# Two transformer layers on one core: gathers that add into x, rows that travel with their weights, an inverse root on VectorE, heads by halves, VectorE in program order in the feed-forward

## The chip, the core and the metric

The kernel runs on one core of a Trainium2 chip. The metric is the device time of one execution in microseconds (us). Six queues matter: TensorE (PE in the profile, its weight loads PEld), VectorE (DVE), ScalarE (ACT), GpSimd (POOL), and the issuing of DMAs by SyncE (SP), ScalarE and POOL. Each works its own instructions in order; semaphores hold an instruction, and all that is queued behind it on the same engine, until its inputs are there.

## The reference

Two pre-norm layers run one after the other on x of shape (2, 1024, 128), float32:

```
x = x + latent_attention(layernorm(x))      # 8 heads, no mask
x = x + experts(layernorm(x))               # 8 experts + 1 shared, top 2 of each token, hidden 352
x = x + causal_attention(layernorm(x))      # 16 heads of 8, rotary
x = x + chosen_mlp(layernorm(x))            # 2 of 8 MLPs for a whole sequence, chosen by its row 0

layernorm(x) = (x - mean) / sqrt(var + 1e-5)
experts(y)   = ffn_shared(y) + sum over the token's 2 experts e of w_e * ffn_e(y)
ffn(y)       = (silu(y @ gate) * (y @ up)) @ down
```

The two weights w_e of a token are its two largest softmax probabilities of the gate, divided by their sum.

## The kernel before

The planner. The kernel is written for a tile framework. It records instructions in program order; then a planner simulates the engines and puts each engine's instructions in an order: an engine that is free takes the ready instruction that is first in program order. `tc.manual_schedule(engines=...)` leaves the named engines in program order instead. Before the change only TensorE is named. Generators make the program order: each `yield` ends a step, `zip_longest` or `beside(main, extras)` takes one step of each generator in turn, `after(n, g)` lets n steps pass first, and `spread(g, n)` makes one step of g into n.

First attention. Four passes' worth of work (2 sequences x 2 groups of 4 heads) run two deep: pass i computes the row maxima of unit i (`maxima0`, scores L513, reduce L517) beside the exponentials and sums of unit i-1 (`attend0`: scores L581 and L587, exp L592, values L612). The sums of exponentials (L597, L600) are formed by POOL, 12 tensors of 128x1024 in each half of a pass; the last unit's by VectorE (`adder`). At the end of a half `den` (L629) needs the sums. Pass i = 3 has 32 steps of this, and beside it `route(0)`; pass 4 has only `attend0(3)`.

`route(b)` prepares the experts of sequence b: layer norm (`layernorm_steps`, keeping the normed rows `xn`), gate logits, softmax, `top2`, ranks of the tokens within their experts (a matmul with a triangle), and from these the place `pos` of each (token, choice) in a list of 23 blocks of 128 rows that is sorted by expert. Then 16 indirect DMAs on POOL (L339; 8 tiles of tokens, 2 choices) scatter the rows `xn` into `xs` in DRAM. All write the same DRAM tile, so each waits for the one before to land. `xs` was filled with zeros at the start.

`layernorm_steps` uses `rsqrt` (L138 to L146): a power of -1/2 on POOL (L140) and one Newton step on VectorE.

Feed-forward. `blocks(b)` runs through the 23 blocks: load (`xb`, L749) of four blocks at a time from `xs`, transpose, then three stages that lie one step apart: `up(j)` (L770, silu L775, product L776), `mid(j-1)` (transposes L783, copy L787), `down(j-2)` (L798, copy to `yb` L803); `yb` goes to `ys` in DRAM by SP (L806). 25 steps. `shared(b)` is the shared expert (L717 to L734), which adds into x. `combine(b)` gathers the two rows of each token from `ys` into one of 6 buffers `yg` (L832, POOL) and adds each, times its weight, into x on VectorE (L841). The order is: blocks(0) with the last quotients of the attention and route(1) beside it; shared(0), blocks(1), shared(1) with `start` (combine(0), heads(0), fetch(0)) and the first maxima of the second attention beside them; then combine(1).

Second attention. `heads(b)` makes layer norm, q and k with rotary, splits each into three bfloat16 parts (copy on ScalarE L915, subtraction on POOL L918) and stores them in `parts` in DRAM by SP (L916). `fetch(i, queue)` loads the operands `qp` and `kp` of head group i from there (L941, 72 rows). `maxima(i)` (L967, reduce L977) finds the row maxima; `send` writes them by way of DRAM into three more rows of qp (`md<-mt` L985, `qp<-md` L986), and `kp` has ones there. `attend(i)` (scores L1065, exp L1070, mask on POOL L1074, values L1090) contracts over all 128 rows, the rest being zeros in qp and ones in kp (memsets L872, L873). Pass i has maxima(i) beside attend(i-1); `choose` picks the MLPs (indirect DMAs L1153 and the bias sum L1163 on POOL), and `finish` does output projection and MLP for half a sequence. `heads(1)` runs beside pass 1.

Of the kernel before, what the change touches and what calls it, by code (L numbers as in the profile page):

```python
# [3 lines left out]

# [6 lines left out]
F32 = mybir.dt.float32  # L11
BF16 = mybir.dt.bfloat16
I32 = mybir.dt.int32
# [24 lines left out]
MASKED = -(2.0 ** 100)  # L38


@with_exitstack
def two_layers(ctx: ExitStack, tc: tile.TileContext, a: dict, out: bass.AP):
# [47 lines left out]
    mhalf = const.tile([P, NT], F32, name="mhalf")  # L90
    nc.vector.memset(mhalf, -0.5)

# [12 lines left out]
    def layernorm_steps(b, bank, xt, keep=None, halves=(0, 1)):  # L105
# [3 lines left out]
        for n in range(4 * halves[0], 4 * halves[-1] + 4):  # L109
            nc.vector.bn_stats(stats[:, n, :], x[:, b * NT + n, :])  # L110
            nc.vector.bn_aggr(mv[:, n, :], stats[:, n, :])
        rstd = rsqrt(mv[:, 4 * halves[0] : 4 * halves[-1] + 4, 1], 4 * len(halves))
        for half in halves:
            xns = []
            for i in range(4):
                n = 4 * half + i
                m = n - 4 * halves[0]
                if keep is None:
                    xn = small.tile([P, D], F32, name="xn", bufs=4)
                else:  # L120
                    xn = keep[:, n, :]
# [4 lines left out]
                xns.append(xn)  # L126
            yield
            tp = bank()
            for i in range(4):
                nc.tensor.transpose(tp[:, i * P : (i + 1) * P], xns[i], ident)  # L130
            h = half - halves[0]
            nc.any.tensor_copy(xt[:, h * 512 : (h + 1) * 512], tp)
        yield

    def rsqrt(v, n):

        var = small.tile([P, n], F32, name="var")
        nc.vector.tensor_scalar(var, v, LN_EPS, None, ALU.add)  # L138
        rstd = small.tile([P, n], F32, name="rstd")
        nc.gpsimd.tensor_tensor(rstd, var, mhalf[:, 0:n], ALU.pow)  # L140

        fix = small.tile([P, n], F32, name="fix")
        nc.vector.tensor_mul(fix, rstd, rstd)
        nc.vector.tensor_mul(fix, fix, var)
        nc.vector.tensor_scalar(fix, fix, -0.5, 1.5, ALU.mult, ALU.add)
        nc.vector.tensor_mul(rstd, rstd, fix)  # L146
# [58 lines left out]
    xs_d = [tc.dram_tile([NBLK * P, D], F32, name=f"xs{b}") for b in range(B)]  # L205
# [42 lines left out]
    def route(b, bank):  # L248


        xn = rt.tile([P, NT, D], F32, name="xn")
        xt = xt_pool.tile([P, S], F32, name="xt")
        yield from layernorm_steps(b, bank, xt, xn)
        lg = bank()[:, 0 : NT * NE].rearrange("p (n e) -> p n e", e=NE)
        for n in range(NT):
            nc.tensor.matmul(
                lg[:, n, :], xt[:, n * P : (n + 1) * P], gate_w, start=True, stop=True
            )
        top = small.tile([P, NT], F32, name="lmax")
# [76 lines left out]
        routed[b] = xt, poss, base, vs  # L336
        for n in range(NT):
            for k in range(2):
                nc.gpsimd.indirect_dma_start(  # L339
                    out=xs_d[b],  # L340
                    out_offset=bass.IndirectOffsetOnAxis(
                        ap=poss[k][:, n : n + 1], axis=0
# [989 lines left out]
```

## Time and profile before

| what | value |
|---|---|
| three runs | 1080.73, 1082.16 and 1087.71 us; median 1082.16 |
| the profiled execution | 1080.86 us, its span 1079.0 us, mean granted TensorE clock 0.916 |
| TensorE busy | 888.1 us, 82% of the span |
| VectorE, ScalarE, POOL busy | 588.7, 431.5, 399.2 us |
| first layer norm to the last denominator of the first attention | 24.5 to 478.7 us |
| blocks(0) | first expert matmul at 480.1 us |
| blocks(1) | first expert matmul at 599.2 us |
| second attention | first score of attend(0) at 718.4 us |

The span runs from the first to the last instruction of one execution; what the metric has beyond it (1.9 us) lies around it. Busy time leaves out the issuing of DMAs. "Granted clock" is the share of TensorE's full clock that it was given. A line in the profile's order of time has start, duration, engine, source line, operation, tiles and, in brackets, how long the engine stood idle before it and what ended that.

### The profile page before, as it was taken

What the parts mean: (1) busy time and instruction counts of PE and PEld (TensorE: products, weight loads), DVE (VectorE), ACT (ScalarE), POOL (GpSimd) and SP (SyncE); (2) the same over time, 40 slices, a digit from 0 to 9 for tenths busy, and PEclk for the clock granted to TensorE, in tenths of its full rate; (3) what the DMA queues carried; (4) which work ended last, traced back from release to release, by engine and by line L of the source; (5) the groups of instructions that cost most, each with busy time, mean ns of one, the idle gap of its engine ahead of it and who ended that gap; (6) DMA issues with size and microseconds to landing.
All of it is one profiled execution on the core that took longest, in us unless ns stands there. A gap on an engine that the chain in (4) does not pass through costs nothing.

```text
span 1079.0 us, 14251 instructions
## 1 busy us (share of the span) xinstructions
PE 888.1 (82%) x5244; PEld 422.4 (39%) x5244; DVE 588.7 (55%) x1060; ACT 431.5 (40%) x720; POOL 399.2 (37%) x491
## 2 busy tenths in 40 slices
PE   3999999999978776996993889768558898879984
PEld 2423353433323222334762556333224344434333
DVE  3496554555665843666512432586436676647532
ACT  0103334443422332653530345115356665656661
POOL 4005546548453573005037141524623321423420
PEclk9899999999988997999896899869769999969998
DMA  9400000000000000012111223303121222130000
GB/s 271 118 1 1 1 2 1 1 1 1 1 1 1 10 20 10 1 30 69 30 52 49 62 81 94 62 17 64 21 60 33 35 37 46 28 44 13 3 1 20
DMA packets 41047, 37.47 MB, mean 35 GB/s; under 512 B 6067, under 2 KB 38227, under 8 KB 39827
## 3 DMA queue, kind: packets, MB, share of 16 engines
q1 hardware_dynamic: 34896, 28.40, 11.4%
q0 software_dynamic: 2848, 5.58, 1.9%
q10 hardware_dynamic: 3235, 2.58, 1.0%
q8 instruction: 42, 0.69, 0.3%
q14 instruction: 26, 0.21, 0.1%
HBM read 24.03 MB, written 12.52 MB: 34 GB/s over the span
## 4 chain that ended last, share of the span: by engine, by line
PE 56%; DVE 16%; POOL 9%; issue 9%; DMA 5%; ACT 3%; POOLq 0%; SPq 0%; ACTq 0%; DVEq 0%
PE sc L581 9%; PE sc L513 7%; PE up L1090 6%; PE ud L612 5%; PE banks L967 5%; DVE mx2a L517 4%; PE bank L1065 4%; PE gub L770 3%; DVE mx L977 3%; POOL xs L339 2%; PE sc L587 2%; DVE rden L639 2%; PE yblk L798 2%; PE den L629 1%; DMA yg<-ys,pos 1%
## 5 line engine op out<-in xcount | busy, mean ns | idle before, releaser
L977 DVE TENSOR_REDUCE mx<-banks 128x2 f32<-128x1024 f32 (+3 forms) x160 | 173.5, 1114 | 85.8 <-PE banks L967 42.7
L592 ACT ACTIVATE ex<-sc 128x1024 f32<-128x1024 f32 x128 | 131.1, 1024 | 218.2 <-PE sc L587 216.0
L517 DVE TENSOR_REDUCE mx2a<-sc 128x2 f32<-128x1024 f32 x128 | 153.7, 1219 | 99.5 <-PE sc L513 92.1
L1070 ACT ACTIVATE ex<-bank 128x512 f32<-128x512 f32 (+2 forms) x320 | 156.6, 557 | 123.2 <-PE bank L1065 115.2
L581 PE MATMUL sc<-q,key 64*128 64x512 f32 x512 | 141.8, 617 | 20.6 <-DVE mx2a L517 20.4
L600 POOL TENSOR_TENSOR sum<-sum,ex 128x1024 f32<-128x1024 f32 x60 | 140.4, 2354 | 38.9 <-ACT ex L592 38.7
L513 PE MATMUL sc<-key,q 64*128 64x512 f32 x512 | 149.5, 638 | 1.2 <-DVE mx2a L517 1.1
L1065 PE MATMUL bank<-qp,kp 128*128 128x512 bf16 (+3 forms) x384 | 98.0, 343 | 38.7 <-DMA qp<-md 31.1
L1074 POOL TENSOR_SCALAR_AFFINE_SELECT ex<-ex 128x128 f32<-128x128 f32 (+1 forms) x192 | 62.8, 332 | 176.3 <-ACT ex L1070 171.7
L967 PE MATMUL banks<-kp,qp 72*128 72x512 bf16 (+3 forms) x384 | 107.2, 351 | 17.8 <-DVE mx L977 14.9
L581 PEld LDWEIGHTS sc<-q,key 64*128 64x128 f32 x512 | 49.7, 190 | 89.3 <-issue 44.3
L597 POOL TENSOR_TENSOR sum<-ex,ex 128x1024 f32<-128x1024 f32 x12 | 28.1, 2348 | 144.9 <-ACT ex L592 144.9
L513 PEld LDWEIGHTS sc<-key,q 64*128 64x128 f32 x512 | 48.5, 191 | 70.5 <-issue 41.0
L1090 PE MATMUL up<-ex,vp 128*32 128x512 f32 (+3 forms) x768 | 75.0, 508 | 0.8 <-POOL ex L1074 0.8
L770 PE MATMUL gub<-wall,xbt 128*128 x184 | 66.3, 487 | 5.0 <-DVE hds L776 3.7
L612 PE MATMUL ud<-ex,val 128*32 128x512 f32 x512 | 69.4, 614 | 0.0
L967 PEld LDWEIGHTS <-qp 72*128 72x128 bf16 x384 | 38.9, 104 | 55.1 <-issue 40.8
L776 DVE TENSOR_TENSOR hds<-slb,gub 128x352 f32<-128x352 f32 x46 | 23.7, 519 | 63.3 <-ACT slb L775 63.1
L1065 PEld LDWEIGHTS <-kp 128*128 128x128 bf16 x384 | 32.7, 100 | 62.9 <-DMA qp<-md 33.3
L639 DVE RECIPROCAL rden<-us 128x128 f32<-128x128 f32 x32 | 28.3, 923 | 48.1 <-ACT us L633 48.1
L339 POOL DMA_INDIRECT xs<-xn,pos x32 | 32.0, 1001 | 60.4 <-DMA xs<-xn,pos 28.3
L587 PE MATMUL sc<-mr,onesb 64*128 64x512 bf16 x256 | 52.0, 384 | 0.0
(247 smaller groups left out, 1132.4 us busy)
## 6 DMA issues: line engine op xcount, KB each, us to landing
qp<-parts SPq DMA_DIRECT2D x72, 64.0 KB
kp<-parts SPq DMA_DIRECT2D x63, 64.0 KB
parts<-qk SPq DMA_DIRECT2D x24, 128.0 KB
xs<-zeros SPq DMA_DIRECT2D x10, 256.0 KB
xb<-xs SPq DMA_DIRECT2D x10, 256.0 KB
ys<-yb SPq DMA_DIRECT2D x10, 256.0 KB
wall<-in_ffn_gate_dram SPq DMA_DIRECT2D x1, 1584.0 KB
wall<-in_ffn_up_dram SPq DMA_DIRECT2D x1, 1584.0 KB
```

The lines of the kernel that those rows point to most:

```text
L513: nc.tensor.matmul(sc[:, j, :], qs[i][pr][r, st * P : (st + 1) * P], key2[r, 512 * c : 512 * (c + 1)], start=True, stop=True,)
L517: nc.vector.tensor_reduce(mx2[:, 2 * pr : 2 * pr + 2, st, c], sc, AX.X, ALU.max, negate=True,)
L581: nc.tensor.matmul(sc[:, j, :], key2[r, k * P : (k + 1) * P], qs[i][pr][r, cols], start=True, stop=False,)
L592: nc.scalar.activation(ex, sc, AF.Exp)
L600: adder.tensor_tensor(sums[pr], sums[pr], ex, ALU.add)
L612: nc.tensor.matmul(ud[DC * j : DC * (j + 1), :], val[:, k, :], es[j // 2][:, j % 2, :], start=(k == 0), stop=(k == NT - 1),)
L770: nc.tensor.matmul(gu[:, s, 0:FF], xbs[j // 4][:, (j % 4) * P : (j % 4 + 1) * P], flat[:, bass.ds(e0 + FF * s, FF)], start=True, stop=True,)
L967: nc.tensor.matmul(sc[:, n, 0:w], qp[0:KP, j, s0 : s0 + P], kp[0:KP, j, c0:c1], start=True, stop=not diag,)
L977: nc.vector.tensor_reduce(to, sc[:, :, 0:w], AX.X, ALU.max, negate=True)
L1065: nc.tensor.matmul(sc[:, j, 0:w], kp[:, j0 + j, t0 : t0 + P], qp[:, j0 + j, lo:hi], start=True, stop=True,)
L1070: nc.scalar.activation(ex[:, :, 0:w], sc[:, :, 0:w], AF.Exp, scale=SCALE1)
L1090: nc.tensor.matmul(up[WH * j : WH * (j + 1), lo - c0 :], vps[b][:, k, h : h + WH], es[j], start=(k == 0), stop=end,)
```

## The change

1. `rsqrt` takes a first guess by an integer shift and subtraction, and four Newton steps of three instructions, all on VectorE.
2. `xs` rows are 129 long: the normed row and its weight. `scatter(b)` copies the weights of a choice into column 128 of `xn` and scatters choice by choice. For sequence 0 it stands in pass 4 of the first attention, for sequence 1 behind route(1), two scatters a step.
3. `down` multiplies each row by its weight as it copies y to `yb` (VectorE), and `combine(b, half)` has indirect DMAs that add the gathered rows into x; `yg` and the VectorE additions go.
4. `layernorm_steps` has more steps (`lag=2` in route and heads), and its copies of the transposes run on ScalarE; route(0) starts after 4 steps and takes one step for each of the pass, route(1) starts after 4.
5. `heads(b, half, xt)` works by halves of the sequence, and its stores are issued by ScalarE.
6. VectorE too is in program order in the feed-forward (blocks(0) up to the end of combine(1)).
7. `attend` contracts over 75 rows; qp is not cleared, kp gets its ones in 32 rows, beside the gathers.
8. `xb` has four buffers; the pools of the second attention have `reuse_waits="tile"`.

```diff
+KP = 9 * DH
+ONES = float(np.uint32(0x3F803F80).view(np.float32))
...
-    def layernorm_steps(b, bank, xt, keep=None, halves=(0, 1)):
+    def layernorm_steps(b, bank, xt, keep=None, halves=(0, 1), lag=1):
...
+        for half in halves:
+            for n in range(4 * half, 4 * half + 4):
+                nc.vector.bn_stats(stats[:, n, :], x[:, b * NT + n, :])
+                nc.vector.bn_aggr(mv[:, n, :], stats[:, n, :])
+            if lag > 1:
+                yield
         rstd = rsqrt(mv[:, 4 * halves[0] : 4 * halves[-1] + 4, 1], 4 * len(halves))
+        if lag > 1:
+            yield
...
+        for _ in range(lag):
+            yield
+        for half in halves:
             tp = bank()
...
-            nc.any.tensor_copy(xt[:, h * 512 : (h + 1) * 512], tp)
+            nc.scalar.copy(xt[:, h * 512 : (h + 1) * 512], tp)
         yield

     def rsqrt(v, n):
...
+        half = small.tile([P, n], I32, name="vhalf")
+        nc.vector.tensor_scalar(half, var.bitcast(I32), 1, None, ALU.logical_shift_right)
         rstd = small.tile([P, n], F32, name="rstd")
-        nc.gpsimd.tensor_tensor(rstd, var, mhalf[:, 0:n], ALU.pow)
+        nc.vector.tensor_scalar(
+            rstd.bitcast(I32), half, -1.0, float(0x5F3759DF), ALU.mult, ALU.add
+        )
         fix = small.tile([P, n], F32, name="fix")
-        nc.vector.tensor_mul(fix, rstd, rstd)
-        nc.vector.tensor_mul(fix, fix, var)
-        nc.vector.tensor_scalar(fix, fix, -0.5, 1.5, ALU.mult, ALU.add)
-        nc.vector.tensor_mul(rstd, rstd, fix)
+        for _ in range(4):
+            nc.vector.tensor_mul(fix, rstd, rstd)
+            nc.vector.scalar_tensor_tensor(fix, fix, -0.5, var, ALU.mult, ALU.mult)
+            nc.vector.scalar_tensor_tensor(rstd, fix, 1.5, rstd, ALU.add, ALU.mult)
...
+    def scatter(b, every=1):
+        _, poss, _, vs, xn = routed[b]
+        for k in range(2):
+            nc.gpsimd.tensor_copy(xn[:, :, D], vs[k])
+            for n in range(NT):
                 nc.gpsimd.indirect_dma_start(
                     out=xs_d[b],
+                    out_offset=bass.IndirectOffsetOnAxis(ap=poss[k][:, n : n + 1], axis=0),
                     in_=xn[:, n, :], in_offset=None,
...
+                if n % every == every - 1:
+                    yield
...
                 if i == n - 1:
-                    yield from after(3, route(0, bank0))
-            passes.append(spread(more(), 4 if i < n - 1 else 2))
+                    yield from after(4, route(0, bank0))
+                if i == n:
+                    yield from scatter(0)
+            passes.append(spread(more(), 4 if i < n - 1 else 1))
...
-            nc.any.tensor_copy(ybs[gi][:, j % 4, :], y)
+            nc.vector.tensor_scalar(
+                ybs[gi][:, j % 4, :], y, xbs[gi][:, j % 4, D : D + 1], None, ALU.mult
+            )
...
-    def combine(b):
+    def combine(b, half):
+        poss = routed[b][1]
+        for k in range(2):
+            for n in range(4 * half, 4 * half + 4):
+                nc.gpsimd.indirect_dma_start(
+                    out=x[:, b * NT + n, :], out_offset=None, in_=ys_d[b],
+                    in_offset=bass.IndirectOffsetOnAxis(ap=poss[k][:, n : n + 1], axis=0),
+                    bounds_check=NBLK * P - 1, oob_is_err=True, compute_op=ALU.add,
+                )
+                if n % 2:
+                    yield
...
+    def route1():
+        yield from route(1, bank1)
+        yield from scatter(1, 2)
+
+    with tc.manual_schedule(engines={mybir.EngineType.PE, mybir.EngineType.DVE}):
+        extras = beside(blocks(0), [quotients(), after(4, route1())])
...
-    for qp, kp in qkp:
-        nc.gpsimd.memset(qp[64:P], 0.0)
-        nc.vector.memset(kp[64:P], 1.0)
...
-                    nc.sync.dma_start(parts_d[b][i, k, :, cols], h)
+                nc.scalar.dma_start(parts_d[b][i, k, :, cols], h)
...
+    def both_heads(b):
+        xt = xt_pool.tile([P, S], F32, name="xt")
+        yield from heads(b, 0, xt)
+        yield from heads(b, 1, xt)
...
+    def ones_of_keys():
+        for _, kp in qkp:
+            yield
+            nc.vector.memset(kp[64:96].bitcast(F32), ONES)
+    def start():
+        for _ in zip_longest(combine(0, 0), ones_of_keys()):
+            yield
+        for _ in zip_longest(combine(0, 1), after(4, both_heads(0))):
+            yield
         fetch(0, nc.gpsimd)
         yield
...
+    def results():
+        yield from combine(1, 0)
+        yield from combine(1, 1)
...
-                        sc[:, j, 0:w], kp[:, j0 + j, t0 : t0 + P],
-                        qp[:, j0 + j, lo:hi], start=True, stop=True,
+                        sc[:, j, 0:w], kp[0 : KP + 3, j0 + j, t0 : t0 + P],
+                        qp[0 : KP + 3, j0 + j, lo:hi], start=True, stop=True,
...
-    extras = [after(2, heads(1), 1)]
+    extras = [after(2, both_heads(1), 1)]
```

## Prediction

> **What bounds the kernel now.** I read the page's shares and chain first, then busy time by stretch, the waits of TensorE, and the order of time around each of its long waits.
>
> ```profile
> PE 888.1 (82%) x5244; PEld 422.4 (39%) x5244; DVE 588.7 (55%) x1060; ACT 431.5 (40%) x720; POOL 399.2 (37%) x491
> PE 56%; DVE 16%; POOL 9%; issue 9%; DMA 5%; ACT 3%; POOLq 0%; SPq 0%; ACTq 0%; DVEq 0%
> ```
>
> TensorE sets the end wherever it is fed; 44% of the chain is what it waits for. So a gain is only a removed wait. There are four big ones. The first stands in stretches of equal work: half a pass of the first attention (the times run from one denominator L629 to the next).
>
> ```profile
> 187.00:234.90 47.90, 47.51 (x276) 18.38 (x272) 25.80 (x33) 20.21 (x21) 28.06 (x12) 1.00 0.00 1
> 234.90:281.40 46.50, 44.75 (x269) 16.31 (x264) 28.25 (x41) 18.54 (x20) 28.00 (x12) 1.00 0.01 1
> 281.40:347.60 66.20, 53.76 (x292) 20.00 (x288) 43.37 (x81) 18.77 (x21) 29.78 (x13) 0.90 0.00 1
> 347.60:416.50 68.90, 47.69 (x270) 16.12 (x263) 33.31 (x50) 19.14 (x21) 44.30 (x28) 0.88 0.05 16
> ```
>
> The waits of TensorE in the last two of them, in total, times and longest:
>
> ```profile
> PE sc L581 <- DVE mx2a L517: 12.4, 4, 6.7
> PE den L629 <- POOL sum L600: 15.8, 2, 11.7
> ```
>
> After length come PE, PEld, DVE, ACT and POOL busy in the first fence, then the granted clock. The two halves of pass 3, with route(0) beside them, take 18 and 22 us more than their twins. In the second, POOL has 16 scatters between its 12 sums:
>
> ```profile
> 373.20 0.97 POOL L339 DMA_INDIRECT xs<-xn,pos  x1 [1.56 <-DMA xs<-xn,pos]
> 375.70 0.97 POOL L339 DMA_INDIRECT xs<-xn,pos  x1 [1.53 <-DMA xs<-xn,pos]
> 376.70 2.35 POOL L600 TENSOR_TENSOR sum<-sum,ex 128x1024 f32<-128x1024 f32 x1
> 379.22 1.00 POOL L339 DMA_INDIRECT xs<-xn,pos  x1 [0.17 <-issue]
> ```
>
> A scatter waits for the landing of the one before (1.5 us), and the sums stand behind it in POOL's queue. Second, blocks(0): three memsets sit in VectorE's queue between the layer norm's steps, and TensorE's transposes wait (a line of the order of time, then one of the waits).
>
> ```profile
> 508.65 3.47 DVE L873 MEMSET kp<- 64x4096 bf16 x1 [0.91 <-issue]
> PE bank L130 <- DVE xn L122: 10.0, 1, 10.0
> ```
>
> Third, blocks(1) waits for the last scatter of route(1), which was held up by 16 gathers on the same queue:
>
> ```profile
> 592.06 1.04 POOL L339 DMA_INDIRECT xs<-xn,pos  x1 [0.30 <-issue]
> 594.42 11.01 SPq L749 DMA_DIRECT2D xb<-xs  x4
> 597.41 1.09 PE L756 MATMUL bank<-ident,xb 128*128 128x128 f32 x4 [4.91 <-DMA xb<-xs]
> ```
>
> Fourth, early in the second attention, TensorE idles 24.3 us:
>
> ```profile
> 769.15 0.62 ACT L915 CAST qk<-ta 128x512 bf16<-128x512 f32 x1
> 783.65 1.14 POOL L918 TENSOR_TENSOR ta<-ta,qk 128x512 f32<-128x512 f32 x1
> 787.35 3.31 SPq L916 DMA_DIRECT2D parts<-qk  x4
> 790.75 0.71 SPq L986 DMA_DIRECT2D qp<-md  x1
> 793.34 1.03 PE L1065 MATMUL bank<-qp,kp 128*128 128x512 bf16 x2 [24.29 <-DMA qp<-md]
> ```
>
> The maxima rows (qp<-md) stand in SP's queue behind the stores of heads(1) (parts<-qk), these wait for ScalarE, ScalarE for POOL's subtraction, and that stands behind eight expert gathers and their sum.
>
> **The change, part by part.**
>
> *Pass 3, second half.* The scatters move in program order to pass 4, where VectorE does the sums and POOL is nearly idle (0.25 us busy from 416.5 to 480). But POOL's order is still the planner's, and it fills gaps: of the 16 scatters now, 8 stand after every sum of pass 3 in program order, yet all 16 ran before the twelfth sum. I take it that they are drawn forward again. What changes is that route's steps come closer: the rank matmuls fall in step 17 of 32, not 21, so the first scatter starts about 6 us into the half instead of 19 (366.8 - 347.6). From there to 416.4 POOL needed 49.6 us for 9 sums of 2.35 and 16 scatters, so 28.4 us for the scatters. After: 6 + 12 x 2.35 + 28.4 = 62.6 against 68.9: **-6** (ends: 0, and -22 if they stay out).
>
> *Pass 3, first half.* The layer norm is cut into steps with maxima between them, and its xt copies go to ScalarE. TensorE's longest wait here is 6.7; half of it: **-3** (0 to -7).
>
> *Inverse root.* Now 15 VectorE instructions in place of 5 and a power on POOL. By the 0.20 us from one small one to the next (L143 to L146) that is 3.0 us, where it took 2.8 for 128x8 (598.38 to 601.16) and 2.1 for 128x4. Only the last norm lies bare on the path: **+1** (0 to +4). All twelve Newton steps read two tiles in SBUF, and beside a POOL sum such an instruction takes 2.30 us at L143 and 2.26 at L144 instead of 0.17. There were just two, since POOL has no third sum while VectorE holds TensorE up; I count the same two. [...]
>
> *blocks(0), scatter(1), gathers.* T0 is the first expert matmul (480.1 now). A step of blocks takes 2.19 us. The kp memsets cover half the rows and come after blocks(0), beside gathers; POOL's qp memsets (10.4 us) go. VectorE in program order carries some 18 us of route(1) over 15 steps, 1.2 a step, with 2.19 - 0.8 free in each: no stall. route(1) needs 19 steps before its scatters: 19 x 2.19 + 1.3 (turns) + 4.2 (quotients, transposes, gate) = T0+47, now T0+57. The last yb is stored at 25 x 2.19 + 2 + 4.2 + 3 = T0+64, and the gathers may start. Scatters alone take 2.73 each (536.9 to 564.2, ten), so 6 are out by then and 10 left. Now the planner put four gathers to a scatter; so 16 gathers and 4 scatters at 1.32 (26.4), then five periods of 2.73 to the start of the last: T0+104. From that to the first matmul of blocks(1) is 7.1 (592.06 to 599.17): T0+111, now T0+119.1: **-8**. At one to one it would be T0+96 (-23).
>
> No row shows a gather that adds. Lower end: the plain gather's 1.32. Upper: the scatter's 2.73, since each second add on a tile waits for the first to land; 16 x 2.73 + 13.7 from T0+64, plus 7.1, gives T0+128.5 (+9). I take 1.32: the second add is issued four or more places later, 5.3 us, against 2.6 from issue to use now (565.48 to 568.10). Behind such a wait on POOL stand the other scatters and later the heads' sums; on VectorE the x add of shared(0) (L734) waits for the same gathers, and behind it the products of shared(0) and blocks(1). That is hidden under the scatters: 64 + 26.4 + 3 is before 111. Rows of 516 bytes change zero fill (issued by 35, used from 366), scatter and xb (fetched two groups ahead; only the first is bare): 0 to +3, taken 0. Two copies of the weights on POOL for each batch, 0.2 each by L1015, the second behind one more landing of 1.5: 0 to +4, in the scatters' own chain, taken 0. The weight moves to yb on VectorE, 0.28 instead of ScalarE's 0.27, VectorE being 30 to 45% busy there: 0, or 0.28 a block if not.
>
> *blocks(1) with heads(0), 70 us.* 12 stores go from SP to ScalarE, 0.33 each (L881) = 4 us in 70, ScalarE being under half busy; SP's xb, yb and fetches no longer stand behind them: 0 (-3 to +4).
>
> *shared(1) to attention, 669.7 to 718.4.* 16 products L841 of 0.35 leave a VectorE that is 80% busy at the end, and the gathers' waits for their buffers (710.40, 713.63) go: **-5** (-10 to +6). The pools' finer reuse waits: attention starts there right behind maxima, no wait shows, 0.
>
> *Second attention.* The power wait at 720 (TensorE idle 3.76): **-2** (0 to -4). The 24.3: without stores ahead of it, qp<-md could go at 765 (mt is done at 762.99), and TensorE at 769. But ScalarE too stood still from 769.8 to 784.8 for POOL, and 6 stores' copies stand before the next exponentials. By halves, the last chunk comes at steps 15 and 16 with buffers long free, just ahead of the expert gathers; POOL work left is 7.2 us, so a wait of 8 to 10 stays: **-14** (-22 to +3). [...] Contraction over 75 rows: 128 and 72 rows take the same (343, 351 ns), 0.
>
> Sum: -6 -3 +1 -8 -5 -2 -14 = -37. The profiled execution took 1080.9 (span 1079.0 and 1.9 around it), 1.3 under the median shown: **1044**.
>
> **Rivals.**
> A. The scatters stay out of pass 3: its second half near 47: 16 more, **1028**. For it: program order, sums first where both are ready; against: the 8 drawn forward.
> B. ScalarE goes on waiting for POOL: the 24.3 only change their name, **1058**. For it: 769.8 to 784.8; against: the chunks come earlier than the gathers.
> C. Slow adds, the slower side. With g us per adding gather, VectorE reaches blocks(1)'s first product at T0+64+16g+2 instead of T0+114 (forecast), which binds from g = 3; after blocks(1) POOL has 37 us for 16 (674.5 to the casts of maxima(0) at 711.4), which binds from 2.3. Cost 16(g-3) + 16(g-2.3). At g = 5: 32 + 43, **1119**; slower than now by 1% from g = 4.2. For it: nothing like it was measured; against: 1.32 and 2.73.
> D. It does little: mixing as at +9 and no gain in pass 3: 1044 + 17 + 9 = **1070**, with B over 1080.
>
> **How the numbers follow.** Forecast 0.50, A 0.17, B 0.17, C 0.08, D 0.08. The likeliest time is 1044; its own range, with the ends of B and scatter mixing, is 1022 to 1062. The range that leaves two in ten out reaches to A with one-to-one mixing (1028 - 15) and to D: 1010 to 1074. About 1% (1071 to 1093) can be told from no change. Forecast, A and B are faster, with a tenth of D's and B's mass lost to the middle: faster 0.83, same 0.09, slower 0.08.
>
> **What would show it.** Right: scatters between the sums of the last POOL half-pass again, that half 60 to 65; the next passes as before; no memset in blocks(0) and that stage near 62 instead of 75; blocks(1) first matmul some 111 after T0; the wait on qp<-md under 10; adding gathers 1.0 to 1.3 on POOL. Wrong: POOL idle between sums there (A); ScalarE idle over 12 us before an L1070 with POOL's subtraction named (B); L734 or products in blocks(1) waiting for the gathers for over 10 us (C); scatters still last before blocks(1) at T0+119 (D).

## The result: 36 us slower, and the profile after

The changed kernel takes 1118.1 us (median of four runs, 1118.0 to 1120.0) against 1082.2 for the kernel before: a ratio of 1.032, 95% interval 1.029 to 1.036. The forecast was 1044, and slower had a chance of 0.08. The profiled execution's span went from 1079.0 to 1116.5 us.

Engine shares and the chain of waits, from the page of the kernel after:

```profile
PE 925.0 (83%) x5244; PEld 435.4 (39%) x5244; DVE 605.1 (54%) x1209; ACT 426.8 (38%) x688; POOL 392.4 (35%) x480
PE 56%; DVE 14%; issue 13%; POOL 10%; ACT 3%; DMA 3%; POOLq 0%; SPq 0%; ACTq 0%; DVEq 0%
```

TensorE executes the same 5244 matmuls, but is busy 925 us with them where it was 888. The clock that it was granted fell: on the mean 0.881 in the profiled execution, where it was 0.916. The sum was made by stages, so the two traces are compared by stages. Busy time by stretch, cut at the first expert matmul of blocks(0) (T0), the first of blocks(1), the first score of the second attention, and the end; columns as in the prediction (length, PE, PEld, DVE, ACT, POOL, granted clock, DMA share, GB/s). The kernel before:

```profile
480.09:599.17 119.08, 81.35 (x429) 59.79 (x429) 52.17 (x143) 37.72 (x85) 47.39 (x39) 0.85 0.18 52
599.17:718.44 119.27, 101.39 (x513) 66.71 (x514) 55.31 (x105) 38.67 (x88) 37.26 (x42) 0.90 0.27 65
718.44:1079.00 360.56, 283.18 (x1992) 133.47 (x1990) 202.04 (x366) 195.44 (x382) 113.28 (x291) 0.90 0.17 31
```

The kernel after:

```profile
477.42:603.72 126.30, 82.06 (x430) 59.33 (x430) 49.65 (x149) 32.15 (x64) 41.70 (x34) 0.81 0.21 50
603.72:737.16 133.44, 100.16 (x513) 67.90 (x514) 63.58 (x162) 36.44 (x73) 45.09 (x42) 0.88 0.27 55
737.16:1116.50 379.34, 323.36 (x1992) 146.31 (x1990) 215.08 (x437) 196.47 (x382) 106.53 (x284) 0.82 0.16 29
```

| stage | before | forecast (before and its terms) | after | after over forecast |
|---|---|---|---|---|
| start to T0 | 480.1 | 472.1 (-6 -3 +1) | 477.4 | +5.3 |
| T0 to blocks(1) | 119.1 | 111.1 (-8) | 126.3 | +15.2 |
| blocks(1) to the second attention | 119.3 | 114.3 (-5) | 133.4 | +19.1 |
| second attention to the end | 360.6 | 344.6 (-2 -14) | 379.3 | +34.7 |

The table names the three places to explain. The waits of TensorE in the kernel after (in total, times, longest) give the first hints:

```profile
PE bank L777 <- DMA xb<-xs: 27.0, 2, 24.0
PE den L648 <- POOL sum L619: 18.5, 2, 18.1
...
PE tp_m L999 <- POOL mp L1035: 17.8, 6, 12.1
PE bank L1095 <- DMA qp<-md: 12.1, 5, 3.0
...
PE banks L985 <- DVE hd L744: 10.8, 2, 9.9
```

The stall that was to go has gone: the longest wait for the maxima rows (qp<-md) is 3.0 us, where it was 24.3. But blocks(1) now waits 24.0 for its rows (4.9 before), and two waits of 12.1 and 9.9 us are new.

**T0 to blocks(1).** In order of time, engines mixed:

```profile
553.11 1.55 POOL L853 DMA_INDIRECT x<-ys,pos  x1 [0.31 <-issue]
554.97 1.56 POOL L853 DMA_INDIRECT x<-ys,pos  x1 [0.30 <-issue]
...
567.27 0.69 DVE L755 TENSOR_TENSOR x<-bank,x 128x512 f32<-128x512 f32 x1 [14.73 <-DMA x<-ys,pos]
...
581.61 1.56 POOL L853 DMA_INDIRECT x<-ys,pos  x1 [0.31 <-issue]
583.48 1.07 POOL L358 DMA_INDIRECT xs<-xn,pos  x1 [0.30 <-issue]
...
585.12 0.69 DVE L755 TENSOR_TENSOR x<-bank,x 128x512 f32<-128x512 f32 x1 [11.44 <-DMA x<-ys,pos]
...
596.60 0.97 POOL L358 DMA_INDIRECT xs<-xn,pos  x1 [1.66 <-DMA xs<-xn,pos]
598.94 2.01 SPq L770 DMA_DIRECT2D xb<-xs  x4
```

An adding gather occupies GpSimd for 1.56 us, and the next one starts 1.86 us after it (553.11 to 554.97); a plain one took 1.01 and 1.32. Two plain ones of the kernel before:

```profile
572.16 1.01 POOL L832 DMA_INDIRECT yg<-ys,pos  x1 [0.30 <-DMA yg<-ys,pos]
573.48 1.01 POOL L832 DMA_INDIRECT yg<-ys,pos  x1 [0.31 <-issue]
```

The last scatters stand behind the gathers in the same queue, and blocks(1) behind the last scatter. VectorE's x add (L755) waits for the gathers twice.

**Before the second attention.** Again in order of time:

```profile
702.21 0.29 DVE L112 BATCH_NORM_STATS2 stats<-x 128x6 f32<-128x128 f32 x1 [4.51 <-DMA x<-ys,pos]
...
707.51 0.29 DVE L112 BATCH_NORM_STATS2 stats<-x 128x6 f32<-128x128 f32 x1 [1.31 <-DMA x<-ys,pos]
...
708.13 0.68 DVE L744 TENSOR_TENSOR hd<-sl,gu 96x512 f32<-96x512 f32 x1
...
725.18 1.56 POOL L853 DMA_INDIRECT x<-ys,pos  x1 [0.30 <-issue]
726.21 0.76 POOL L1033 CAST mp<-mx 128x16 bf16<-128x16 f32 x1
...
731.29 0.30 PE L999 MATMUL tp_m<-identb,mp 128*48 128x128 bf16 x1 [12.09 <-POOL mp L1035]
```

On VectorE the statistics of heads(1)'s layer norm stand ahead of the last product of shared(1), and each waits for a gather: that is TensorE's 9.9. On GpSimd the casts of the first maxima (L1033) stand among the gathers: that is the 12.1.

**Second attention.** Stretches of 4 us of the kernel after, early in one of its passes:

```profile
841.00:845.00 4.00, 4.00 (x25) 1.65 (x25) 1.74 (x3) 1.94 (x4) 0.00 (x0) 0.50 0.09 24
845.00:849.00 4.00, 4.00 (x13) 1.52 (x12) 2.82 (x3) 2.54 (x6) 0.00 (x0) 0.50 0.40 69
849.00:853.00 4.00, 4.00 (x20) 0.81 (x18) 1.32 (x2) 1.53 (x3) 0.00 (x0) 0.50 0.55 66
```

And of the kernel before, behind a like wait (its stretch from 890 to 894 has TensorE busy 1.75 of 4):

```profile
894.00:898.00 4.00, 4.00 (x28) 1.65 (x27) 1.86 (x4) 2.36 (x5) 0.00 (x0) 0.57 0.01 0
898.00:902.00 4.00, 2.83 (x19) 1.61 (x18) 3.23 (x6) 2.49 (x5) 0.00 (x0) 1.00 0.22 55
```

After some of its short waits (2.27 us until 839.41, with qp<-md named; 1.93 until 893.44 before the change) the clock falls to 0.50. In the stretch shown of before it was back at 1.00 some 4 us later; now TensorE is busy without a gap for 12 us and still gets 0.50. Counted in such stretches, the clock lies below 0.75 for 140 us of the second attention, where it was 68. This isn't seen as a wait anywhere, but as busy time: 323.4 us against 283.2.

### The profile page after: what moved, and what is told of

It is laid out like the page before. It is cut to its first block, busy times and chain, and to the rows that moved or that the text cites. A ratio compares the mean times of both kernels' runs of the same rounds, so it can differ in the third digit from the quotient of the medians.

```text
span 1116.5 us, 14367 instructions
## 1 busy us (share of the span) xinstructions
PE 925.0 (83%) x5244; PEld 435.4 (39%) x5244; DVE 605.1 (54%) x1209; ACT 426.8 (38%) x688; POOL 392.4 (35%) x480
## 4 chain that ended last, share of the span: by engine, by line
PE 56%; DVE 14%; issue 13%; POOL 10%; ACT 3%; DMA 3%; POOLq 0%; SPq 0%; ACTq 0%; DVEq 0%
PE sc L600 9%; PE sc L532 7%; PE up L1120 7%; PE bank L1095 6%; PE banks L985 5%; PE ud L631 5%; DVE mx2a L536 4%; POOL x L853 4%; PE sc L606 2%; DVE mx L995 2%; DVE rden L658 2%; POOL xs L358 2%; POOL ta L930 2%; PE gub L791 1%; PE den L648 1%
## 5 line engine op out<-in xcount | busy, mean ns | idle before, releaser
L995 DVE TENSOR_REDUCE mx<-banks 128x2 f32<-128x1024 f32 (+3 forms) x160 | 174.6, 1114 | 91.1 <-PE banks L990 67.9
L985 PE MATMUL banks<-kp,qp 72*128 72x512 bf16 (+3 forms) x384 | 116.8, 377 | 16.0 <-DVE hd L744 10.8
L1095 PE MATMUL bank<-qp,kp 75*128 75x512 bf16 (+3 forms) x384 | 108.7, 374 | 20.4 <-DMA qp<-md 12.1
L1120 PE MATMUL up<-ex,vp 128*32 128x512 f32 (+3 forms) x768 | 89.6, 579 | 2.8 <-POOL ex L1104 2.8
L853 POOL DMA_INDIRECT x<-ys,pos x32 | 50.3, 1571 | 45.7 <-DVE x L755 37.0
L985 PEld LDWEIGHTS <-qp 72*128 72x128 bf16 x384 | 41.1, 109 | 57.8 <-issue 44.5
L1095 PEld LDWEIGHTS <-kp 75*128 75x128 bf16 x384 | 35.5, 108 | 49.9 <-issue 22.7
L990 PE MATMUL banks<-mask_st,identb 128*128 128x128 bf16 x256 | 53.6, 237 | 0.0
```

What stands on the lines that cost most here:

```text
L853: nc.gpsimd.indirect_dma_start(out=x[:, b * NT + n, :], out_offset=None, in_=ys_d[b], in_offset=bass.IndirectOffsetOnAxis(ap=poss[k][:, n ...
L985: nc.tensor.matmul(sc[:, n, 0:w], qp[0:KP, j, s0 : s0 + P], kp[0:KP, j, c0:c1], start=True, stop=not diag,)
L995: nc.vector.tensor_reduce(to, sc[:, :, 0:w], AX.X, ALU.max, negate=True)
L1095: nc.tensor.matmul(sc[:, j, 0:w], kp[0 : KP + 3, j0 + j, t0 : t0 + P], qp[0 : KP + 3, j0 + j, lo:hi], start=True, stop=True,)
L1120: nc.tensor.matmul(up[WH * j : WH * (j + 1), lo - c0 :], vps[b][:, k, h : h + WH], es[j], start=(k == 0), stop=end,)
```

## Experiments

Two theories came from this. **K**: contracting the scores over 75 rows in place of 128 keeps the granted clock low for longer. **G**: the adding gather's own time is the cost in the middle. Their rivals: the clock falls because the waits have moved (I), and VectorE in program order is the cost (V).

### K against I: the rows alone, taken from the one kernel and given back to the other

```diff
 # before.py, L1065 (e1); after.py the other way round (e2)
-sc[:, j, 0:w], kp[:, j0 + j, t0 : t0 + P], qp[:, j0 + j, lo:hi]
+sc[:, j, 0:w], kp[0 : KP + 3, j0 + j, t0 : t0 + P], qp[0 : KP + 3, j0 + j, lo:hi]
```

Kernel before with 75 rows, expected:

> The kernel before, with the scores of the second attention contracted over 75 rows in place of 128 and nothing else changed (the rows left out hold zeros, so the result stays). Theory K: fewer rows keep the granted TensorE clock at 0.50 for longer after each wait of the second attention (after the change it stays there 12 to 16 us, before 4 to 8), so the time rises by 25 to 40 us, to 1107 to 1122, and the mean granted clock from 718 us on falls from near 0.92 to near 0.82. Rival I: the clock falls because of the changed waits, rows have no part in it: within 5 us of 1082.

Kernel after with 128 rows, expected:

> The kernel after, with the scores of the second attention contracted over all 128 rows again (VectorE's memsets of the keys cover rows 64 to 128, and three more, of zeros into the queries, stand beside them, where VectorE waits anyway). Theory K: the time falls by 25 to 40 us, to 1078 to 1093; the stall of 24 us that the change removed stays removed. Rival I (rows have no part in the clock): 1113 to 1123.

Measured: 1112.5 us (ratio to before 1.027, 1.023 to 1.030), so +30; and 1089.2 (1.005, 1.003 to 1.008), so -29 from the kernel after. The first one's windows show the same picture as the kernel after, with nothing else of the change in it:

```profile
838.00:842.00 4.00, 4.00 (x26) 1.66 (x22) 1.91 (x3) 2.04 (x5) 0.00 (x0) 0.50 0.10 24
842.00:846.00 4.00, 4.00 (x13) 1.52 (x11) 2.45 (x3) 2.52 (x5) 0.00 (x0) 0.50 0.39 71
846.00:850.00 4.00, 4.00 (x19) 0.61 (x17) 1.23 (x1) 1.08 (x2) 0.00 (x0) 0.50 0.53 64
```

K holds and I falls. With 128 rows the second attention of the changed kernel takes 348.2 us, 12.4 less than before the change, and TensorE is busy 291.2 us in it: of the 40 us of added busy time the rows account for 32.

### How the loss depends on the rows

The same line with 104, 88 and 96 rows, on the kernel before:

> The kernel before with the scores of the second attention contracted over 104 rows (rows left out hold zeros). If the loss grows with the rows left out (53 of 128 cost 30 us): 24 rows cost some 14, 1092 to 1100. If it comes at once with any row left out: 1107 to 1115. If 104 is enough for the clock: 1080 to 1086.

> The kernel before with the scores of the second attention contracted over 88 rows (rows left out hold zeros). If the loss sets in at once when 96 rows or fewer are used: 1107 to 1115. If it fades between 75 (1112.5) and 104 rows (1084.9) in proportion: 1096 to 1102. If it begins only below 88: 1081 to 1087.

> As the kernel beside it, with 96 rows. If the loss sets in at once when 96 rows or fewer are used: 1107 to 1115. In proportion between 75 and 104: 1090 to 1094. If it begins below 96: 1081 to 1087.

| rows | time, us | ratio to before (95%) |
|---|---|---|
| 75 | 1112.5 | 1.027 (1.023 to 1.030) |
| 88 | 1100.9 | 1.020 (1.014 to 1.025) |
| 96 | 1086.6 | 1.006 (1.003 to 1.009) |
| 104 | 1084.9 | 1.001 (0.999 to 1.002) |

104 rows cost nothing that can be measured, 96 about 5 us, 88 about 19 with runs from 1091 to 1107, 75 all 30. On the mean the loss fades out between 75 and 104 rows. 88 rows lie in the range named for a loss in proportion, 96 in the one named for hardly any. The traces show how the mean comes about, in stretches of 1 us: TensorE is busy throughout and yet at 0.50 for at most 6 us on end with 128 rows (kernel before), 8 with 104, 7 with 96, and 15 with 88 and with 75 (e1). With 88 rows some of these stretches are as short as with 128 (3 us from 838) and one as long as with 75 (15 us from 798).

### G against V: the gathers and VectorE's order

`e4` gives VectorE's order in the feed-forward back to the planner; `e3` does so too and gathers plainly, with the sums on VectorE.

```diff
-with tc.manual_schedule(engines={PE, DVE}):          # e3 and e4, twice
+with tc.manual_schedule(engines={PE}):
-    out=x[:, b * NT + n, :], ..., compute_op=ALU.add,   # e3 only
+    out=y, ...,
+nc.vector.tensor_add(x[:, b * NT + n, :], y, x[:, b * NT + n, :])
```

> The kernel after with plain gathers into buffers of their own and the sums on VectorE (weights stay in the rows), and with VectorE's order in the feed-forward left to the planner again. Theory G (the adding gather is the cost: 1.86 us from one to the next against 1.32, and its read and write of x ties it to the sums of the shared expert): the first expert matmul of blocks(1) comes 10 to 20 us earlier than now, shared(1) to attention takes about 50 in place of 62, and the time is 1085 to 1095, at least 8 below the kernel that frees VectorE's order alone. Rival V (VectorE in program order is the cost): within 5 us of that kernel.

> The kernel after with VectorE's order in the feed-forward left to the planner again, the gathers adding as they do. Theory G: blocks(1) still waits for scatters that stand behind the adding gathers on POOL, so only the wait of the layer norm's statistics ahead of the products in shared(1) goes, 10 us: 1104 to 1112. Rival V (VectorE in program order is the cost): the waits at both ends of blocks(1) go, 1090 to 1098.

Measured: e4 1122.6 (ratio to before 1.036, 1.032 to 1.039), 4.5 over the kernel after and no gain at all; e3 1091.4 (1.005, 1.002 to 1.009), 31 below e4. The 4.5 lie before T0 (482.4 against 477.4), which this edit doesn't reach; each stage behind it is within 0.3 us of the kernel after. V falls: program order was no loss. G had expected a small gain from e4 and was wrong in that: TensorE's wait of 9.9 for a product is gone, but one of 10.5 for the first maxima (PE banks L985 <- DVE mx L995) stands in its place.

What of the adding gather costs, its own time or the waits that come with writing x in place? `e13` drops the addition and keeps every wait (it is e2 with one more edit, so it stands against e2's 1089.2):

```diff
-    bounds_check=NBLK * P - 1, oob_is_err=True, compute_op=ALU.add,
+    bounds_check=NBLK * P - 1, oob_is_err=True,
```

> The kernel after with 128 rows (1089.2 us) and with gathers that overwrite x and do not add to it: the sum of the shared expert and of the first gather is left out of the result, every wait on x stays. If the instruction's own time is the cost: the gathers follow each other at 1.3 us, 16 x 0.54 = 9 us go in front of blocks(1) and as many in front of the second attention, 1069 to 1074. If the waits on x are the cost: 1083 to 1091.

Measured: 1068.6, so -20.6. Groups of GpSimd in the middle stage, first the kernel after, then e13 (columns: busy us, mean ns, idle before and its reasons):

```profile
L853 POOL DMA_INDIRECT x<-ys,pos x16 | 25.1, 1570 | 4.7 <-issue 4.7
```

```profile
L853 POOL DMA_INDIRECT x<-ys,pos x16 | 16.5, 1031 | 4.7 <-issue 4.4 <-DMA xs<-xn,pos 0.3
```

The time is lost in the instruction: 0.54 us in each of 32. In e13 blocks(1) starts 117.0 us after T0, against 125.9 with the addition (-8.9), and the next stage takes 124.3 against 133.6 (-9.3); 16 x 0.54 is 8.6. The other 3 us of the gain fall in the second attention (345.1 against 348.2) and are not explained.

### Both parts undone

The edits of e2 and e3 together are `e5b`; `e5a` is the same, but keeps VectorE in program order.

> The kernel after with both parts that proved costly undone: contraction over 128 rows, and plain gathers with the sums on VectorE, VectorE still in program order in the feed-forward. If the two losses (29 us for the rows, 27 to 31 for the adding gathers) lie in different stages and add up: 1058 to 1066, faster than the kernel before by 16 to 24. If program order makes VectorE wait for the plain gathers just as it waited for the adding ones: 1078 to 1090.

> As the kernel beside it, with VectorE's order in the feed-forward left to the planner. If the two losses add up: 1058 to 1066. If they overlap (the stall at the start of the second attention comes back when attention starts earlier): 1075 to 1090.

Measured: with VectorE in program order 1063.8 (0.984, 0.979 to 0.990), left to the planner 1068.9 (0.988, 0.983 to 0.994). With program order the two losses add up, and without them the change is a gain of 18 us. Left to the planner it is 3 over the range for that: blocks(1) starts 124.6 us after T0 there, 113.9 with program order. The better of the two is still 20 short of the forecast.

### The scatters of batch 0 (rival A)

`e6` is e5b with GpSimd added to the engines in program order, in passes 3 and 4 each by itself. The scatters stayed in pass 3 (the first at 355.7, the last at 405.6), since each pass keeps an order of its own, so 1069.9 us says nothing on A. `e8` is e5a with passes 3 and 4 under one order:

```diff
-for each pass: with tc.manual_schedule(engines={PE}): ...
+passes 3 and 4 together: with tc.manual_schedule(engines={PE, Pool}): ...
```

> The free kernel beside it, with GpSimd in program order in passes 3 and 4 of the first attention, so that the 16 scatters of batch 0 stay in pass 4, where GpSimd has no sums. The prediction priced this as rival A at 16 us (22 at most): 14 to 22 below the kernel beside it, the second half of pass 3 at 47 to 50 us, no wait of the denominators for the sums. Against it: if pass 3 is held by VectorE's maxima and not by GpSimd, under 5; if 16 scatters at 2.7 us (43) end after pass 4 has (60), nothing is lost there.

> The kernel with 128 rows and plain gathers (VectorE in program order in the feed-forward, 1063.8 us), now with GpSimd in one program order over passes 3 and 4 together, so that the 16 scatters of batch 0 come after the last sum of pass 3. (With an order for each pass by itself they stayed in pass 3: first at 355.7, last at 405.6.) Rival A as the prediction priced it: the wait of 19.3 us before a denominator goes, the second half of pass 3 takes 47 to 50 us, the time is 14 to 20 lower, 1044 to 1050. Against A: the sums end last only because VectorE's maxima and the sums share the half anyway: under 5 lower.

Measured: 1047.6 (0.968, 0.962 to 0.974), 16.3 below the same kernel without it. The two halves of pass 3 and then pass 4, e8:

```profile
280.40:345.10 64.70, 52.81 (x294) 20.29 (x289) 44.76 (x89) 19.79 (x23) 28.14 (x12) 0.92 0.00 1
345.10:397.40 52.30, 47.00 (x267) 17.18 (x263) 30.34 (x50) 18.49 (x20) 30.22 (x15) 0.93 0.01 2
397.40:455.70 58.30, 58.30 (x382) 20.12 (x378) 37.59 (x42) 35.34 (x37) 17.93 (x16) 1.00 0.06 18
```

The second half drops from 66 to 52, and pass 4 hides the 16 scatters. The price of rival A was right.

### The stores on ScalarE, alone and undone

One line, `nc.sync.dma_start(parts_d...)` to `nc.scalar.dma_start(parts_d...)`, put into the kernel before (e7) and taken out of the kernel after (e7b):

> The kernel before with one change: the 24 stores of the head parts are issued by ScalarE and not by SyncE. If the stall of 24.3 us at the start of the second attention is the maxima rows standing behind these stores in SyncE's queue, it shrinks to 10 us or less and the time falls by 14 to 22 us, to 1060 to 1068. If an issuing engine changes nothing but its own issue time: 1078 to 1084. If ScalarE, which waits for GpSimd's subtraction, is the real holder, the stall stays over 15 under another name: 1073 to 1080.

> The kernel after with one part undone: the stores of the head parts are issued by SyncE again. If the heads by halves took the stall at the start of the second attention away by themselves: 1115 to 1121, the longest wait for the maxima rows under 5 us. If it was the queue: that wait is 10 to 25 us again and the time 1126 to 1140.

Measured: e7 1060.4 (0.981, 0.975 to 0.986), -22 from one line; e7b 1134.5 (1.048, 1.044 to 1.053), +16, of which 12.9 lie in the second attention (392.2 against 379.3) and 4.1 before T0, which this line doesn't reach. The wait for the maxima rows, e7 and then e7b:

```profile
PE bank L1065 <- DMA qp<-md: 11.5, 5, 2.8
```

```profile
PE bank L1095 <- DMA qp<-md: 30.1, 5, 20.0
```

So this line is what counts, and the heads by halves do not remove the stall without it. How it does so is shown in part. In e7b, as in the kernel before, the stores stand in SyncE's queue ahead of the maxima rows and wait for ScalarE (waits of that queue from 740 to 840 us):

```profile
SPq L928 <- ACT qk L927: 55.5, 10, 27.5
```

But in both pairs the planner orders GpSimd differently too. With the stores on ScalarE its last four subtractions come ahead of the expert gathers (e7: the last at 757.3, gathers from 768.7; after: 789.3, gathers from 790.6), with the stores on SyncE behind them (before: from 783.7, gathers from 768.2; e7b: from 812.9, gathers from 796.8). That takes ScalarE's wait away as well. What the queue alone is worth, with GpSimd's order kept, was not run.

### Two tries that failed

`e9`: e7, with the memsets of the keys' rows on GpSimd.

```diff
-nc.vector.memset(kp[64:P], 1.0)
+nc.gpsimd.memset(kp[64:P], 1.0)
```

> The kernel before with the stores of the parts on ScalarE (1060.4 us) and, besides, the three memsets of the keys' rows on GpSimd in place of VectorE. If these memsets are what holds the layer norm of route(1) (TensorE waits 10.0 us once): that wait goes, blocks(0) takes about 10 less, the scatters of route(1) start 10 earlier and blocks(1) with them, 1048 to 1053. If they only move the wait onto GpSimd or the scatters then stand behind 21 us of memsets: 1058 to 1064.

Measured: 1066.4 (0.985, 0.980 to 0.990), 6 slower than e7, of which 2.4 lie before T0, which the edit doesn't reach; it is no gain. In order of time, GpSimd and VectorE:

```profile
506.44 3.53 POOL L872 MEMSET qp<- 64x4096 bf16 x1
507.07 6.58 DVE L122 TENSOR_SCALAR xn<-x,mv,rstd 128x128 f32<-128x128 f32 x3
...
510.73 10.19 DVE L122 TENSOR_SCALAR xn<-x,mv,rstd 128x128 f32<-128x128 f32 x5
```

In e7 the eight scalings of the layer norm were one line:

```profile
513.35 2.14 DVE L122 TENSOR_SCALAR xn<-x,mv,rstd 128x128 f32<-128x128 f32 x8 [0.24 <-DVE rstd L146]
```

Beside GpSimd's memsets they take 13.8 us, from 507.07 to 520.92 (the two entries above overlap). The memset left VectorE's queue and stopped it all the same.

`e11`: both parts undone, the planner's order for VectorE, and GpSimd in program order from blocks(0) on, all 16 scatters of batch 1 ahead of the gathers.

```diff
-with tc.manual_schedule(engines={PE}): blocks(0) ...
-with tc.manual_schedule(engines={PE}): rest of the feed-forward ...
+both together: with tc.manual_schedule(engines={PE, Pool}): ...
-yield from scatter(1, 2)
+yield from scatter(1, 8)
```

> The free kernel with 128 rows and plain gathers (1068.9 us), now with GpSimd in program order from blocks(0) on and all 16 scatters of batch 1 ahead of the gathers. If what blocks(1) waits for is scatters that stand behind gathers on GpSimd: its first expert matmul comes near 109 us after that of blocks(0) in place of 124.6. The time then falls by 8 to 14, to 1055 to 1061, if VectorE's sums of the later gathers don't hold its products; by under 5 if they do.

Measured: 1076.2 (0.996, 0.993 to 0.998), 7 slower than e5b. blocks(1) does start 109.2 us after T0, as expected. But its products stand on VectorE behind the sums of the gathers, now the last in line:

```profile
588.50 0.29 DVE L859 TENSOR_TENSOR x<-yg,x 128x128 f32<-128x128 f32 x1 [21.63 <-DMA yg<-ys,pos]
```

What blocks(1) won at its start (15.4 us) the next stage lost: 135.7 us against 119.2 in e5b. TensorE's waits for the products of blocks(1), 1.0 us in e5b, are 7.1 of that:

```profile
PE bank L804 <- DVE hds L797: 7.1, 3, 6.0
```

### The version that beats both

`e12` is the kernel before with the two parts that paid, the stores on ScalarE and the scatters of batch 0 behind the sums (which the change wrote there, and the planner drew forward), and with the six memsets of the rows writing 32-bit words.

```diff
-nc.sync.dma_start(parts_d[b][i, k, :, cols], h)
+nc.scalar.dma_start(parts_d[b][i, k, :, cols], h)
-for each pass: with tc.manual_schedule(engines={PE}): ...
+passes 3 and 4 together: with tc.manual_schedule(engines={PE, Pool}): ...
+if i == n: yield from scatter(0)          # no longer at the end of route(0)
-nc.gpsimd.memset(qp[64:P], 0.0); nc.vector.memset(kp[64:P], 1.0)
+nc.gpsimd.memset(qp[64:P].bitcast(F32), 0.0); nc.vector.memset(kp[64:P].bitcast(F32), ONES)
```

> The kernel before with the two parts that the runs showed to pay: the stores of the parts on ScalarE (22 us alone), and the scatters of batch 0 behind the last sum of pass 3, with GpSimd in one program order over passes 3 and 4 (16 us on the changed kernel). The six memsets of the keys' and queries' rows besides write 32-bit words (half as many). If the rest of the change (heads by halves, VectorE's order, the inverse root, weights with the rows) gives nothing that the two don't: 1039 to 1046. If the rest holds a gain of its own: 1050 to 1058, above the 1047.6 of the changed kernel with its two bad parts undone and the scatters in pass 4.

Measured: 1033.7 us, ratio 0.953 (0.950 to 0.955), 48 us faster than before and 14 faster than e8, which holds the rest of the change. This is below both ranges named. e8 loses 4.4 us before T0, 1.7 from there to blocks(1) and 5.7 from blocks(1) to the second attention (121.6 against 115.9); the second attention is alike (346.9, 346.4). What part of the rest costs this was not taken apart. Nor were the memsets run alone: from T0 to blocks(1) e12 takes 112.5 us, e7 119.1, and neither the stores nor the scatters of batch 0 lie there. TensorE's longest wait for xn fell from 10.0 to 5.4.

## Why the prediction was wrong, point by point

**Contraction over 75 rows, taken as 0: +31.** This is the largest error. The step compared durations of matmuls with 128 and 72 rows (343 and 351 ns) and found them equal. That holds at a given clock (two matmuls of 512 columns take 0.60 us with 128 rows and 0.61 with 75 at 1.00, and 1.06 with either at 0.50); it says nothing on which clock is granted while such matmuls run. The second attention takes 379.3 us, and 348.2 with all rows. The rest of this stage was right: forecast 344.6, and with 128 rows 3.6 over it.

**The adding gather, taken at the plain one's 1.32 us: it is 1.86 (9 us before blocks(1), 9 behind).** This is inside the bounds given (1.32 to 2.73), but the price put on it failed. The forecast's own sum has 16 gathers and 4 scatters one after another on the path (26.4 us), so each us more of a gather is on the path at once: 16 x 0.54 = 8.6. Rival C nevertheless let it bind only from 3 us, because it looked at VectorE's wait for the gathers and not at the scatters behind them in GpSimd's queue; its "slower from 4.2 us" followed from that. The sign named for C, VectorE waiting over 10 us for the gathers, did come (14.7 and 11.4), but it was not what cost. For the second stage it gave GpSimd 37 us of room and let it bind from 2.3 us; the 9.3 us there came at 1.86.

**route(1) to the scatters, T0+47: it was T0+56.** The 2.19 us are a step of blocks alone. Over blocks(0) a step took 2.68 on the mean (59.0 us from T0 to the last up-projection's start, 22 steps), since TensorE also does transposes, gate and quotients between them. 19 x 2.68 + 4.2 is 55. The gathers, too, started at T0+70.5 and not T0+64. With the last five scatters of 2.6 the rest is as worked out: 70.5 + 35.6 + 13.1 + 7.1 = 126.3.

**What was right in that stage and bought nothing.** No memset in blocks(0), and its last up-projection starts 59.0 after T0 in place of 69.9. VectorE's x add waits for the gathers (14.7 and 11.4 us) and this is hidden under the scatters, as said. Rows of 516 bytes cost the scatter nothing (0.98 us, 2.63 from one to the next; before 0.97 and 2.73). The gain in blocks(0) is lost because blocks(1) waits for GpSimd's queue, not for blocks(0).

**Pass 3, -6 and -3: -2.4 and -1.2.** The scatters are drawn forward again, as forecast: the first starts 7.9 us into the half, not 19. That is 1.9 later than forecast, and 12 sums with 16 scatters then took 58.6 us and not 56.6, with four sums left for the end (401.4 to 410.6): 66.5 in place of 62.6. Stretches of the kernel after that answer to those shown of before:

```profile
184.40:232.70 48.30, 47.90 (x280) 18.52 (x276) 25.79 (x33) 20.60 (x22) 28.04 (x12) 1.00 0.00 1
232.70:279.20 46.50, 44.75 (x272) 16.33 (x268) 28.26 (x41) 18.53 (x20) 28.02 (x12) 1.00 0.00 1
279.20:344.20 65.00, 52.73 (x296) 20.18 (x292) 45.15 (x89) 19.83 (x23) 28.21 (x13) 0.92 0.00 1
344.20:410.70 66.50, 46.03 (x271) 16.07 (x263) 30.19 (x50) 19.30 (x21) 44.35 (x29) 0.87 0.05 17
```

The passes without route are as before. T0 came 2.7 earlier, but 2.1 of that were there already at the denominator that begins these stretches (184.4, before 186.5), and no edit gave them: near the start TensorE waited 3.0 us for w_o in this execution, 5.9 before, and in e2, e4, e7b and e13, which are alike up to T0, T0 came at 479.9 to 482.4. From that denominator to T0 it takes 293.0 us, before 293.6. What pass 3 won was lost again, since the first xb is now fetched at 472.8, after the last denominators, and TensorE waits 3.0 us for it, where it didn't wait before. The sum had 0 to +3 for the longer rows and took 0; that they are what delays this fetch isn't shown.

**The inverse root.** Two instructions in the norm of pass 3 take longer beside sums of GpSimd, as many as were counted: 2.30 us at L150, which reads one tile, and 2.26 at L155, a Newton step. The other eleven of the four steps take 0.17 each.

**shared(1) to attention, -5.** Gathers of 1.86 took 9.3 of the 19 us by which this stage missed. The rest, statistics and casts that stand behind gathers on VectorE and GpSimd, is read from the trace (9.9 and 12.1 us in all, the gathers' own time within them) and was not tried by itself.

**The stall of 24.3 us, -14.** Right in size: the second attention with all rows takes 12.4 less, and one line alone gives 22. That the queue's order decided it is argued, since GpSimd's order changed with that line. Issue time alone doesn't account for it: at the 0.33 us that one store takes to issue on ScalarE (L916 in e7) the 24 are 8 us, an estimate, and e7 gave -22, e7b +16. Rival B did not come. Rival A's price was met once the scatters did stay out (16.3), rival D's cause (mixing) was a part of what happened in the middle.

## What to carry to other kernels

Equal durations of single matmuls don't make two shapes equal for the stage (343 and 351 ns here, and 31 us between them): look at the granted clock behind each short wait, and at busy time that grows with an unchanged count (283.2 to 323.4 us for 1992 matmuls). Here a longer instruction on a queue cost its excess times its count (16 x 0.54 is 8.6, measured 8.9 and 9.3) where something on the path stood behind it in that queue, whatever its own result was needed for. And try the parts of a large change one by one: two of these gave 22 and 16 us, two took 29 and 21, and the best kernel is the old one with the first two and shorter memsets (GpSimd's three take 5.3 us in it, 10.4 before).

## What the runs showed of the hardware and the planner

- The clock granted to TensorE changed with the rows that the scores use: from the second attention on it is 0.91 on the mean with 128 rows (e2) and 0.82 with 75 (the kernel after), 0.90 in the kernel before and 0.81 with 75 rows in it (e1). With 75 rows it stayed at 0.50 over 12 us in which TensorE was busy without a gap, with 128 it was at 0.50 for 2 to 6 us of such work (kernel before). 104 rows are as good as 128 (1.001 of the time), 96 nearly (1.006). How the rows enter isn't shown here.
- An indirect gather that adds into its destination holds GpSimd for 1.57 us, the same gather that overwrites for 1.03. The second add on a tile, four gathers behind the first, showed no wait for its landing (0.3 us idle, as between any two).
- Beside GpSimd's memsets (3.5 us each) VectorE's scaling of 128x128 tiles in SBUF takes longer: eight take 13.8 us in e9, 2.14 in e7. Why isn't shown here.
- An order by hand holds within its block only. Two blocks one after another left the planner free to move GpSimd's scatters from the second into the first (e6), and one block around both did not (e8).
